# GpSimd copies of convolution weights, a last row point in written order, and another order of row points in a Winograd-style attention kernel

## The chip, the cores and the metric

The kernel runs on one core of a Trainium2 chip. The metric is the device time of one execution in microseconds (us), as the median of several runs. The core has engines with a queue each: TensorE (PE in the profile), VectorE (DVE), ScalarE (ACT), GpSimd (POOL), and SyncE (SP), which here issues most of the DMA transfers.

## The reference

The input x has 4 images of 256 channels and 64 x 64 pixels. A 7x7 convolution with dilation 2 (256 to 128 channels) and a 1x1 convolution (128 to 49) give 49 logits per pixel. A softmax over them weights the 49 shifted pixels of x. The sum is then whitened in groups of 64 channels over all images.

```python
k = lax.conv_general_dilated(x, w1, window_strides=(1, 1), padding=[(6, 6), (6, 6)], rhs_dilation=(2, 2), dimension_numbers=DN) + b1[None, :, None, None]
k = lax.conv_general_dilated(k, w2, window_strides=(1, 1), padding=[(0, 0), (0, 0)], dimension_numbers=DN) + b2[None, :, None, None]
attn = jax.nn.softmax(k, axis=1)
xp = jnp.pad(x, ((0, 0), (0, 0), (6, 6), (6, 6)))
shifts = jnp.stack([xp[:, :, 2 * u:2 * u + x.shape[2], 2 * v:2 * v + x.shape[3]] for u in range(7) for v in range(7)], axis=1)
return jnp.einsum('bkchw,bkhw->bchw', shifts, attn)
...
Sigma = EPS * I + jnp.einsum('gdm,gem->gde', xc, xc) / m
rTr = (1.0 / jnp.einsum('gii->g', Sigma))[:, None, None]
Sigma_N = Sigma * rTr
P = I
for _ in range(T_ITERS):
    P3 = jnp.einsum('gij,gjk,gkl->gil', P, P, P)
    P = 1.5 * P - 0.5 * jnp.einsum('gij,gjk->gik', P3, Sigma_N)
wm = P * jnp.sqrt(rTr)
xn = jnp.einsum('gde,gem->gdm', wm, xc)
```

## The kernel before

**The convolution.** The two convolutions are folded into one with 49 outputs, and that is computed in the manner of Winograd (Toom): in each direction the seven taps and the pixels are evaluated at seven points (0, 1, -1, 2, -2, one more, and infinity, which has the number 6 and the name `INF`), multiplied point by point, and interpolated. The outer loop runs over images and their *row points*, in the order of `ROWS` (L29). For one row point, the seven *column points* go in three groups, `BANKS` (L26): 1, 2, 0, then 3, 4, infinity, then 5. Each finite row point costs 96, 80 and 32 matmuls for the three banks; infinity has half the weights and so half the matmuls.

For one row point the steps are these. `row_eval` (L432) evaluates the pixels in the row direction on DVE (into one of three buffers `rb`), with some copies on ACT. `col_ops` (L466) evaluates that in the column direction into the tiles `xh`, one per column point, each of them single: the xh of the next row point can be written only when PE has read that of this one. `weights` (L361) makes the weights `wr0`, `wr1`, `wr2` of the banks: when a row point is used for the first time they are computed from the row-evaluated weights (DVE, with the points 0 and infinity as plain copies on ACT at L405, L406 and L415, and scalings on ACT at L428) and stored to `gd` in DRAM; after that they are loaded from `gd` by a DMA on SP's queue. The tiles wr0 to wr2 have one buffer each. The kept row-evaluated weights of row points 4, 5 and infinity come back by a DMA into `rb[0]`. `conv_bank` (L513) does the matmuls of one bank, and ACT copies their PSUM to `pv` (L541). `col_interp` (L602) interpolates `pv` in the column direction into `zz`, on DVE; `row_interp` (L633) interpolates the seven `zz` in the row direction into the logits `lgx`, in two parts: the first when all row points but the last are there, the second after the last.

`conv_step(k, i)` (L705) runs one bank: matmuls of row point k, then `prepare` (L697) for the same bank of row point k + 1, then the interpolation of k behind its last bank.

**Images.** Image 0 takes row points 1, 2, 3 and direct convolutions for the others; image 1 has infinity by a direct convolution and takes 0 to 5; images 2 and 3 take all seven. So the weights of rows 0, 4 and 5 are first made in image 1, and those of infinity in image 2.

**Softmax and attention.** While the convolution of image b runs, PE also does the softmax transposes of image b - 1 and the attention of an earlier image in *halves*: each has pixel transposes (L975, L1036), copies of them by ACT to `xb` (L983) and `yt` (L1044), and band matmuls (L1004). The softmax weights are exponentials on ACT (L860), maxima `mx`, reciprocals `s`, masks `rm` and products `d` on DVE (L852 to L873), copied to `zt` (L906), stored by SP to `sd` and loaded back as `band` (`load_band`, L937), which DVE transposes in place (L957). `plan` and `gap` (L1158 to L1210) place these between conv steps: a row of image b + 1 counts 6, 5 and 2 units for its banks (infinity half of that), and after each eighth of an image's units one gap's work is issued.

**What sets the order.** PE runs in the order in which the program is written (`pe` keeps it). The other engines' queues are ordered by a scheduler, with two means to fix it: `tc.high_priority()`, and `in_order()` (L293), under which the DVE instructions issued through `in_turn` (L280) form a strict chain and have high priority. The later part of a step can slip ahead of the earlier one where neither holds. Before, `in_order()` holds for the interpolation of row 4 (with the first part of `row_interp`) and of row 5, but not for `prepare`.

Of the kernel before, what the change touches and what calls it, by code (L numbers as in the profile page):

```python
# [23 lines left out]
INF = 6  # L24
# [1 line left out]
BANKS = ((1, 2, 0), (3, 4, 6), (5,))  # L26
ORDER = sum(BANKS, ())

ROWS = (INF, 0, 1, 2, 3, 4, 5)  # L29


@with_exitstack
def kernel(
# [29 lines left out]
    nc = tc.nc  # L63
    B, C, H, W = x.shape
# [24 lines left out]
    def taps(b):  # L89
        return (0,) if b == INF else (0, 1)  # L90
# [203 lines left out]
    @contextmanager  # L294
    def in_order():
        was = strict[0]
        strict[0] = True
        with tc.high_priority():
            yield
        strict[0] = was  # L300

    def add(o, a, b):
        return in_turn(TT(o, a, b, ALU.add))  # L303

    def sub(o, a, b):
        return in_turn(TT(o, a, b, ALU.subtract))  # L306

    def madd(o, a, f, b):

        return in_turn(STT(o, a, f, b, ALU.mult, ALU.add))  # L310
# [50 lines left out]
    def weights(b, br, i, mid=None):  # L361

        first = (br, i) not in made
        made.add((br, i))
        s0 = slot_of[BANKS[i][0]]
        ns = sum(len(taps(bc)) for bc in BANKS[i])  # L370
        nk = NSK * len(taps(br)) // 2
        wt = apool.tile([P, ns, NSK], F32, tag=f"wr{i}", name=f"wr_{b}_{br}_{i}")[:, :, :nk]
        w = {bc: wt[:, slot_of[bc] - s0 : slot_of[bc] - s0 + len(taps(bc))] for bc in BANKS[i]}
        if not first:
            nc.sync.dma_start(wt, gd[br][:, s0 : s0 + ns])
            return w

        if br == 0:
            g = [gr0[:, v] for v in range(KS)]
        elif br in kept:  # L380

            f = rb[0].rearrange("p q r c w -> p (q r c w)")[:, : KS * nk]
            if i == 0:
                nc.sync.dma_start(f, kept[br])
            f = f.rearrange("p (v a r k) -> p v a r k", v=KS, a=NCC, k=KT)
            g = [f[:, v] for v in range(KS)]
        else:
            g = [gbr[:, v] for v in range(KS)]
        g = [t.rearrange("p a r k -> p (a r k)") for t in g]

        e = ct.rearrange("p a b -> p (a b)") if b else store[4].rearrange("p c r w -> p (c r w)")
        e, o, e1 = (e[:, k * nk : (k + 1) * nk] for k in range(3))
        g0 = [g[KS - 1 - a] for a in range(4)]
        g1 = [g[KS - 5 - a] for a in range(3)]
        o0 = {bc: w[bc][:, 0] for bc in w}
        o1 = {bc: w[bc][:, 1] for bc in w if bc != INF}
        if i == 0:
            add(e, g0[0], g0[2])
            add(o, g0[1], g0[3])
            add(e1, g1[0], g1[2])  # L400
            add(o0[1], e, o)
            sub(o0[2], e, o)
            add(o1[1], e1, g1[1])
            sub(o1[2], e1, g1[1])
            nc.scalar.copy(o0[0], g0[0])  # L405
            nc.scalar.copy(o1[0], g1[0])  # L406
        elif i == 1:
            madd(e, g0[2], 4.0, g0[0])
            madd(o, g0[3], 4.0, g0[1])
            madd(e1, g1[2], 4.0, g1[0])  # L410
            madd(o0[3], o, 2.0, e)
            madd(o0[4], o, -2.0, e)
            madd(o1[3], g1[1], 2.0, e1)
            madd(o1[4], g1[1], -2.0, e1)
            nc.scalar.copy(o0[INF], g0[3])  # L415
        else:
            madd(o0[5], g0[0], 2.0, g0[1])
            madd(o1[5], g1[0], 4.0, g1[2])
            madd(o0[5], o0[5], 2.0, g0[2])
            if mid is not None:  # L420
                mid()
            madd(o1[5], g1[1], 2.0, o1[5])
            madd(o0[5], o0[5], 2.0, g0[3])
            add(o1[5], o1[5], o1[5])
        for bc in BANKS[i]:
            f = SCALE[bc] * (SCALE[br] if br not in kept else 1.0)
            if f != 1.0:
                nc.scalar.mul(w[bc], w[bc], f)  # L428
        nc.sync.dma_start(gd[br][:, s0 : s0 + ns], wt)
        return w  # L430

    def row_eval(b, br, rb=rb):  # L432

        for pr in range(2):
            xs = slots[2 * b + pr].rearrange("p c (q a) w -> p a q c w", a=4)
            r = [t[:, :, pr] for t in rb]
            if br == 1:
                add(r[0], xs[:, 0], xs[:, 2])
                add(r[1], xs[:, 1], xs[:, 3])
            elif br == 0:  # L440
                nc.scalar.copy(r[2], xs[:, 0])
            elif br == INF:
                nc.scalar.copy(r[1], xs[:, 3])
            X = [[xs[:, a, :, cc] for a in range(4)] for cc in range(NCC)]
            q = [[t[:, :, cc] for t in r] for cc in range(NCC)]
            for cc in range(NCC):
                if br == 3:
                    madd(q[cc][1], X[cc][2], 4.0, X[cc][0])
                    madd(q[cc][2], X[cc][3], 4.0, X[cc][1])
                elif br == 5:  # L450
                    madd(q[cc][2], X[cc][0], 2.0, X[cc][1])
            for a in (2, 3) if br == 5 else ():
                for cc in range(NCC):
                    madd(q[cc][2], q[cc][2], 2.0, X[cc][a])
        r = [t.rearrange("p q r c w -> p (q r c w)") for t in rb]
        if br == 1:
            add(r[2], r[0], r[1])
        elif br == 2:
            sub(r[0], r[0], r[1])
        elif br == 3:  # L460
            madd(r[0], r[2], 2.0, r[1])
        elif br == 4:
            madd(r[1], r[2], -2.0, r[1])
        return rb[{1: 2, 2: 0, 3: 0, 4: 1, 5: 2, 0: 2, INF: 1}[br]]
# [30 lines left out]
    def col_eval(src, i):  # L495
        for _ in col_ops(src, i):
            pass

    def both0(src, br, i):

        g = col_ops(src, i)
        next(g)
        nxt.update(weights(0, br, i, lambda: next(g)))
        for _ in g:
            pass
# [96 lines left out]
    def col_interp(b, br, part=None):  # L602
        at = slot[b, br]
        pt = {
            c: pv[:K2, at, i].rearrange("p q b -> p (q b)").rearrange(
                "p (q b two) -> p q b two", q=Q9, two=2
            )
            for i, c in enumerate(ORDER)
        }
        outs = phases(zz[:K2, br].rearrange("p q (w two) -> p q w two", two=2))  # L610
        cut = lambda t, k: t[:, :, k : k + Q8]
        if b > 0:

            t = pv[:K2, (at + 2) % NV, NP - 1].rearrange("p q b -> p (q b)")
        else:
            t = ct.rearrange("p a b -> p (a b)")[:K2, :PT]
        interpolate(
            pt, t.rearrange("p (q b two) -> p q b two", q=Q9, two=2), outs, cut, part
        )

        def end():
            ins = nc.scalar.copy(outs[3], cut(pt[5], 0))
            if br == INF:

                nc.gpsimd.memset(zz[:, INF, Q8], 0.0)
            return ins

        if part is None and b > 0 and br != ROWS[-2]:
            later.append(end)
        elif part != 0:  # L630
            end()
# [58 lines left out]
    nc.vector.memset(acc, 0.0)  # L690
    rows = [(0, br) for br in (1, 2, 3)]
    NR0 = len(rows)
    rows += [(b, br) for b in range(1, B) for br in ROWS[1 if b == 1 else 0 :]]
    cur, nxt = {}, {}

    def prepare(k, i):

        b, br = rows[k]
        w = weights(b, br, i)
        if i == 0:  # L700
            cur["x"] = row_eval(b, br)
        nxt.update(w)
        col_eval(cur["x"], i)

    def conv_step(k, i):  # L705
        w = {bc: nxt.pop(bc) for bc in BANKS[i]}
        b, br = rows[k]
        conv_bank(b, br, i, w)
        end = b > 0 and br == ROWS[-1]
        if end:  # L710

            with in_order():
                if i == len(BANKS) - 2:
                    col_interp(b, br, 0)
                elif i == len(BANKS) - 1:
                    col_interp(b, br, 1)
                    row_interp(b, 1)
        if k + 1 < len(rows):
            prepare(k + 1, i)
        if i == len(BANKS) - 1 and not end:  # L720
            last = br == ROWS[-2]
            with in_order() if last else nullcontext():
                col_interp(b, br)
                if last:
                    row_interp(b, 0)
# [24 lines left out]
    for i in three:  # L750
        nxt.update(weights(0, 1, i))
# [678 lines left out]
```

## Time and profile before

| | us |
|---|---|
| Median of 3 runs (lowest to highest) | 763.97 (761.77 to 764.57) |
| The profiled execution's own time | 761.8 |
| Its span, first to last instruction | 760.0 |
| PE busy | 698.6 (92%) |
| DVE busy | 643.0 (85%) |
| ACT busy | 342.8 (45%) |
| POOL busy | 33.7 (4%) |
| PE idle ahead of infinity bank 1 of image 2 (303.48) | 3.55 |
| PE idle ahead of infinity bank 2 of image 3 (460.68) | 7.34 |
| PE idle behind a late xb (277.62) | 4.32 |

The busy times and the span come from the profile of one execution, the idle times from its timeline. In a line of the timeline the first number is the start and the second the length, both in us, then come engine, line of the kernel, operation, output and inputs with their shapes, and in brackets the idle time of the engine before it with what ended that. A group of waits gives the same as a sum over the execution.

### The profile page before, as it was taken

The numbers are of one execution on the slowest core, as the hardware profiler recorded it, in microseconds if no ns is written. First come the engines' busy times: TensorE is split into PE (matmuls) and PEld (weight loads), VectorE is DVE, ScalarE is ACT, GpSimd is POOL, SyncE is SP. The second block draws the span as 40 slices with busy tenths as digits, with TensorE's granted clock in tenths as the row PEclk, the third lists the DMA queues.
The fourth block names the chain that finished last, engine by engine and source line by source line (L and its number), as shares of the span: only waits on it lengthen the run. The fifth ranks groups of instructions, "written<-read, shape, count | busy, mean of one in ns | idle before, by whom it ended". The sixth has DMA issues, their size and how long they took to land.

```text
span 760.0 us, 18845 instructions
## 1 busy us (share of the span) xinstructions
PE 698.6 (92%) x7608; PEld 539.3 (71%) x7608; DVE 643.0 (85%) x1394; ACT 342.8 (45%) x980; POOL 33.7 (4%) x45
## 2 busy tenths in 40 slices
PE   6999999996999877999999977999999889998996
PEld 1459643376998766888998967998898668885322
DVE  3799899999999989999994999999979675545665
ACT  1414240255355726366545442745435473322464
POOL 0410000020000010002000100000000000000000
PEclk9999999999899989999999998999999999999999
DMA  8981120227163563246745731342532134363488
GB/s 323 254 293 72 60 86 0 87 98 233 33 220 120 198 216 88 80 141 217 226 137 184 233 105 47 126 111 91 165 90 79 50 98 140 117 232 136 191 357 338
DMA packets 62911, 115.39 MB, mean 152 GB/s; under 512 B 26295, under 2 KB 45416, under 8 KB 62056
## 3 DMA queue, kind: packets, MB, share of 16 engines
q1 hardware_dynamic: 59128, 95.31, 38.4%
q0 software_dynamic: 3696, 18.88, 7.2%
q8 instruction: 60, 0.98, 0.6%
q14 instruction: 27, 0.22, 0.1%
HBM read 66.18 MB, written 47.98 MB: 150 GB/s over the span
## 4 chain that ended last, share of the span: by engine, by line
DVE 44%; PE 41%; ACT 5%; DMA 4%; issue 4%; SPq 1%; DVEq 0%; ACTq 0%
PE cv L531 9%; PE y L1004 8%; PE acc L668 6%; DVE xh L310 6%; DVE pv L310 5%; DVE rb L310 4%; PE tp L1370 4%; DVE ct L310 3%; DVE band L957 3%; DVE ct L303 3%; DVE zz L310 3%; DVE pv L306 2%; PE tp L1036 2%; PE tp L975 2%; PE sig L1057 2%
## 5 line engine op out<-in xcount | busy, mean ns | idle before, releaser
L531 PE MATMUL cv<-xh,wr 128*49 128x128 f32 (+1 forms) x4576 | 268.8, 279 | 19.5 <-issue 7.3
L531 PEld LDWEIGHTS cv<-xh,wr 128*49 128x49 f32 x4576 | 260.6, 126 | 25.5 <-issue 18.0
L1004 PE MATMUL y<-band,xb 128*128 128x224 f32 (+2 forms) x640 | 151.2, 374 | 15.0 <-ACT xb L983 12.9
L1004 PEld LDWEIGHTS y<-band,xb 128*128 128x128 f32 x640 | 109.6, 193 | 36.4 <-ACT xb L983 16.0
L541 ACT COPY pv<-cv 113x486 f32<-113x486 f32 (+1 forms) x69 | 33.2, 483 | 101.8 <-PE cv L531 101.5
L1023 ACT ACTIVATE slot<-y,pivot 128x512 f32<-128x512 f32 x53 | 36.8, 741 | 62.1 <-PE y L1004 62.1
L310 DVE SCALAR_TENSOR_TENSOR pv<-pv 113x162 f32<-113x162 f32 x215 | 63.8, 318 | 0.5
L1044 ACT COPY yt<-tp 128x256 f32<-128x256 f32 x128 | 45.9, 379 | 36.3 <-PE tp L1036 35.2
L957 DVE STREAM_TRANSPOSE band<-band 128x960 f32<-128x960 f32 (+1 forms) x48 | 50.9, 1060 | 9.9 <-DMA band<-sd 9.9
L1036 PE MATMUL tp<-ident,slot 128*128 128x128 f32 x256 | 52.0, 299 | 4.4 <-ACT yt L1044 2.3
L975 PE MATMUL tp<-ident,slot 128*128 128x128 f32 x256 | 50.5, 300 | 4.6 <-ACT yt L1044 4.5
L1036 PEld LDWEIGHTS tp<-ident,slot 128*128 128x128 f32 x256 | 41.3, 205 | 13.3 <-issue 3.2
L975 PEld LDWEIGHTS tp<-ident,slot 128*128 128x128 f32 x256 | 40.4, 206 | 11.0 <-ACT yt L1044 6.0
L906 ACT COPY zt<-d 32x112 f32<-32x112 f32 (+2 forms) x156 | 45.0, 289 | 1.8
L860 ACT ACTIVATE d<-tp,mx 128x49 f32<-128x49 f32 x128 | 37.5, 335 | 14.0 <-DVE mx L855 10.7
L310 DVE SCALAR_TENSOR_TENSOR xh<-ct 128x512 f32<-128x512 f32 x46 | 30.3, 683 | 10.2 <-PE cv L531 10.2
L1057 PE MATMUL sig<-yt 128*64 128x65 f32 x1024 | 36.9, 225 | 0.0
L1057 PEld LDWEIGHTS sig<-yt 128*64 128x64 f32 x1024 | 32.5, 137 | 6.0 <-issue 4.5
L983 DVE COPY xb<-tp 128x256 f32<-128x256 f32 x41 | 16.4, 421 | 23.7 <-PE tp L975 23.7
L983 ACT COPY xb<-tp 128x256 f32<-128x256 f32 x87 | 30.4, 376 | 12.7 <-PE tp L975 12.0
L306 DVE TENSOR_TENSOR pv<-pv 113x162 f32<-113x162 f32 x112 | 34.6, 319 | 0.4
L668 PE MATMUL acc<-slot,tap 128*49 128x496 f32 (+3 forms) x168 | 34.6, 569 | 0.0
(221 smaller groups left out, 947.2 us busy)
## 6 DMA issues: line engine op xcount, KB each, us to landing
out_dram<-out SPq DMA_DIRECT2D x32, 512.0 KB, 3.4
sd<-zt SPq DMA_DIRECT2D x16, 896.0 KB, 4.2
slot<-in_x_dram POOLq DMA_DIRECT2D x12, 1024.0 KB, 9.2
band<-sd SPq DMA_DIRECT2D x128, 84.0 KB, 2.2
wr<-gd SPq DMA_DIRECT2D x15, 588.0 KB, 3.8
wr<-gd SPq DMA_DIRECT2D x15, 490.0 KB, 3.5
spill<-slot POOLq DMA_DIRECT2D x3, 2048.0 KB, 8.4
back<-spill SPq DMA_DIRECT2D x3, 2048.0 KB, 12.8
```

What stands on the lines that cost most here:

```text
L306: return in_turn(TT(o, a, b, ALU.subtract))
L310: return in_turn(STT(o, a, f, b, ALU.mult, ALU.add))
L531: nc.tensor.matmul(cv[h * HB : h * HB + KT, k, sr : sr + n, sc : sc + n], wv[:, sc, sr, cc], xh[bc][:, :n, h * NCC + cc, :n], start=(j == ...
L668: nc.tensor.matmul(ps[h * HB : h * HB + KT, :, w0:w1_], w[v][:, cc], xs[:, :, cc, w0 + d : w1_ + d], start=(j == 0), stop=(j == len(order) ...
L906: ins = nc.scalar.copy(o, i)
L957: nc.vector.transpose(f, f)
L975: nc.tensor.transpose(t[:, cc * P : (cc + 1) * P], xt[:, cc, CR * m : CR * (m + 1), bass.ds(pc, SW, 2)], ident,)
L983: (nc.vector.tensor_copy if tail else nc.scalar.copy)(xb, t[:, :C])
L1004: nc.tensor.matmul(ps[:, cc, q0 - half * HALF : q1 - half * HALF, :], xb[:, cc * P : (cc + 1) * P], rhs, start=(k == 0), stop=(k == len(PI ...
L1036: nc.tensor.transpose(t[:, cc * P : (cc + 1) * P], yt[:, cc, CR * i : CR * (i + 1), bass.ds(pc, SW, 2)], ident,)
L1044: nc.scalar.copy(yb.rearrange("p a g c -> p (a g) c")[:, :, :GW], t[:, :C].rearrange("p (e c) -> p e c", c=GW),)
L1057: nc.tensor.matmul(sig[g * GW : (g + 1) * GW, cc], yb[:, cc, g, :GW], yb[:, cc, g], start=(count[0] == 0 and cc == 0), stop=(count[0] == 4 ...
```

## The change

The change has three parts. `ROWS` begins with row point 0 and has infinity second; image 1 still leaves infinity out, so its own order (0, 1, 2, 3, 4, 5) stays, and images 2 and 3 take 0, infinity, 1, 2, 3, 4, 5 where they took infinity, 0, 1, 2, 3, 4, 5. The plain copies of weights are issued on GpSimd in images 1 and later, and stay on ScalarE in image 0. And `prepare` for row point 5, banks 1 and 2, is put under `in_order()` in images 1 to 3: these instructions join the strict chain, so that they stand ahead of the interpolation of row 4, which is issued after them.

```diff
-ROWS = (INF, 0, 1, 2, 3, 4, 5)
+ROWS = (0, INF, 1, 2, 3, 4, 5)
...
+
+        same = nc.scalar.copy if b == 0 else nc.gpsimd.tensor_copy
         if i == 0:
...
-            nc.scalar.copy(o0[0], g0[0])
-            nc.scalar.copy(o1[0], g1[0])
+            same(o0[0], g0[0])
+            same(o1[0], g1[0])
         elif i == 1:
...
-            nc.scalar.copy(o0[INF], g0[3])
+            same(o0[INF], g0[3])
...
-    rows += [(b, br) for b in range(1, B) for br in ROWS[1 if b == 1 else 0 :]]
+    rows += [(b, br) for b in range(1, B) for br in ROWS if (b, br) != (1, INF)]
...
         if k + 1 < len(rows):
-            prepare(k + 1, i)
+
+            with in_order() if b > 0 and br == ROWS[-2] and i > 0 else nullcontext():
+                prepare(k + 1, i)
```

## The prediction

> **What bounds the kernel now.** I read the page first, for the engines' shares and the chain that ended last.
>
> ```profile
> PE 698.6 (92%) x7608; PEld 539.3 (71%) x7608; DVE 643.0 (85%) x1394; ACT 342.8 (45%) x980; POOL 33.7 (4%) x45
> ...
> DVE 44%; PE 41%; ACT 5%; DMA 4%; issue 4%; SPq 1%; DVEq 0%; ACTq 0%
> ```
>
> PE is busy 92% of the span, yet the chain lies on DVE as often as on PE: the limit changes from stage to stage. ACT has room. So I asked next for busy time in stretches around the places that the change touches.
>
> ```profile
> 280.00:300.00 20.00, 18.42 (x226) 16.41 (x222) 16.87 (x48) 11.61 (x27) 0.00 (x0) 0.92 0.22 49
> 300.00:340.00 40.00, 35.45 (x462) 33.00 (x463) 40.00 (x82) 21.36 (x76) 0.15 (x1) 0.96 0.38 115
> ...
> 400.00:420.00 20.00, 19.47 (x282) 17.79 (x280) 9.37 (x16) 10.68 (x29) 0.57 (x1) 1.00 0.59 210
> 420.00:460.00 40.00, 31.72 (x410) 28.08 (x406) 39.00 (x84) 17.97 (x37) 3.38 (x2) 0.97 0.51 145
> 460.00:480.00 20.00, 19.32 (x238) 18.22 (x240) 19.97 (x40) 6.18 (x17) 0.00 (x0) 0.90 0.15 42
> ```
>
> The columns are length, then busy time of PE, weight loads, DVE, ACT and POOL, clock, DMA share and GB/s. Around the change of image (image 2 begins at about 297 us, image 3 at about 447) DVE is full and PE has holes. From 400 to 420 it is the reverse. The timeline of PE shows the holes.
>
> ```profile
> 277.62 1.17 PE L1004 MATMUL y<-band,xb 128*128 128x96 f32 x4 [4.32 <-ACT xb L983]
> ...
> 303.48 4.12 PE L531 MATMUL cv<-xh,wr 128*49 128x128 f32 x40 [3.55 <-DVE xh L310]
> ...
> 323.38 12.11 PE L531 MATMUL cv<-xh,wr 128*49 128x128 f32 x208
> ```
>
> The last line is rows 0 (banks 1 and 2) and 1 (bank 0) of image 2 in one go: 80 + 32 + 96 matmuls. The first 112 take 12.11 x 112/208 = 6.5 us, so row 1 of image 2 starts at about 330.0. Image 3 has the like hole (7.34 us, before 460.68), and its row 1 starts at 477.33 + 11.80 x 112/208 = 483.7. The timelines of ACT and DVE show who holds whom:
>
> ```profile
> 276.85 0.27 ACT L405 COPY wr<-rb 128x98 f32<-128x98 f32 x1 [5.10 <-DMA rb<-gi]
> ...
> 277.20 0.36 ACT L983 COPY xb<-tp 128x256 f32<-128x256 f32 x1
> ```
> ```profile
> 282.94 1.18 DVE L957 STREAM_TRANSPOSE band<-band 128x960 f32<-128x960 f32 x1 [3.52 <-DMA band<-sd]
> ...
> 329.22 0.63 DVE L303 TENSOR_TENSOR xh<-ct 128x512 f32<-128x512 f32 x1
> ...
> 416.54 0.69 DVE L310 SCALAR_TENSOR_TENSOR xh<-ct 128x512 f32<-128x512 f32 x1 [6.30 <-PE cv L531]
> ...
> 481.64 0.68 DVE L303 TENSOR_TENSOR xh<-ct 128x512 f32<-128x512 f32 x1
> ```
>
> ACT's weight copy for infinity waits 5.10 us for the kept weights; the copy of xb behind it comes late, PE idles 4.32 us, and the band that follows is late for DVE (3.52 us). After that DVE runs without a hole, and the first xh of row 1 is ready at 329.8 (image 2) and 482.2 (image 3), just when PE needs it. What the change is worth is therefore how far it moves these two starts; from each of them on the PE order of both kernels is the same and DVE is some 6 to 11 us ahead.
>
> [...]No run here shows a 128x196 copy on POOL; the nearest row is the swap copy 128x64, two in 0.41 us.[...]
>
> **Part 1, copies to POOL.** Twelve copies leave ACT: rows 0, 4 and 5 of image 1 (nine of 128x196, .36 to .38 us each) and infinity of image 2 (three of 128x98, .27): 9 x .37 + 3 x .27 = 4.1 us of ACT. ACT is 45% busy, so that itself is worth nothing, except where a copy holds the queue: the 5.10 us wait now stands on POOL, where only a spill and slot loads stand near it (issued at 258.96 and 268.07, ahead of infinity's copies). It gives back up to 3.5 us on DVE plus a .19 us band wait at 299.76: 3.7. On POOL I estimate .27 us for a copy 128x196 and .18 for 98 wide. Row 0's three fall near 100 us, where PE is full (39.08 of 40 from 60 to 100) and covers them. The other nine (6 x .27 + 3 x .18 = 2.2) fall where DVE is the limit[...]. I take .4, as the copies wait for the same DMA as DVE's first weight instruction and mostly overlap waits.
>
> **Part 2, row 0 first.** No instruction is added or removed in images 2 and 3. PE now runs row 0 (banks 0, 1), the attention half and softmax transposes, row 0 bank 2, infinity (48 + 40 + 16 matmuls), then row 1. Row 1's evaluation (four of 1.13 us and one of 2.2), and the softmax pieces mx, s, rm and d of the image before, now come on DVE between infinity's and row 1's xh. Adding up every DVE instruction from row 5 of image 1 to row 1 of image 2 by its duration from the timeline gives 72.0 us before and 72.3 after: +.3. So the hole of PE ahead of infinity bank 2 isn't filled: it moves ahead of row 1, and is about 10 us there, since PE then has less conv work (infinity, half as wide) ahead of it. Row 1's start is still DVE's queue.
>
> New waits stand in that queue, all bounded by zero below: mx waits for the softmax transposes, which PE reaches later than DVE does (0 to .9 us, from PE's transposes ending near 309.8 in my schedule); the second reciprocal waits for exponentials that stand on ACT behind eleven zt copies (3.40 us in one group) and an eviction (0 to 1.1); bands of the next half wait for a transfer (0 to 1.9 for two). One more band transpose (1.09) now stands between row 1's first and second xh; PE needs the second 1.8 us (32 matmuls at 12.11/208 = .058) after the first, so it is just covered (.6 + 1.1 = 1.7); if its load is late, every us of it shows.
>
> **Part 3, row 5 in strict order.** The evaluation for row 5, banks 1 and 2, is put on the written order in images 1 to 3, ahead of the interpolation of row 4. It adds waits: xh is single, so its bank 2 must wait for PE to have read that of row 4, and the interpolation, bands and row_interp queue behind it. Before, those pieces slipped in between. Image 1: 0 to 1.0 us (bank 2 of row 4 ends near 262.7). Image 2: it falls in the stretch where DVE is idle half the time (9.37 of 20) and PE full; nothing, and without that cover some .5. Image 3 has no row after row 5, so its own end isn't touched.
>
> **Sum.** Image 2's row 1: -3.7 (wait gone) + .3 (order) + .4 (POOL) + half to all of the new waits, of 4.9 in all (.9 + 1.1 + 1.9 + 1.0); I take 3.4: +.4. Image 3: the strict wait .4, mx and reciprocal .4 to .9 each at half: from 0 to +1.0; +.5. Total about +.9: the profiled execution, 761.8 (span 760.0 and 1.8 around it), would become 762.7. The median of the runs shown is 2.2 above that execution, so 764.9 in its terms, no change that can be told: 0.5%, 3.8 us, is about what a measurement can tell.
>
> **Rivals.** *Faster, the holes are reclaimed.* If none of the new waits appears and PE's earlier start on image 2 lets the bands arrive early, image 2 gains the full 3.7 and about 1 us of strict order (row 5's conv starting earlier in image 1, where PE idles 2.22 us at 254); image 3, whose 1.0 us of DVE idling from 420 to 460 goes, .8 more: -5.5, 758.5. For it: the waits of before are measured, the new ones estimated. Against it: DVE is full from 300 to 400 and 420 to 540, and a full queue can't be shortened by order. *Much faster*: DVE's queue isn't what sets row 1, and the 4.3 and 7.3 us of PE become conv work: -11.6, 752.4. Against: xh at 329.22 and 481.64 ends where PE starts.
>
> *Slower, a band takes the place of the wait.* SP issues the bands in order behind weight loads and stores that wait for PE; wr tiles are single, so row 1's weight load waits for infinity's conv. The band transpose between row 1's two xh then waits on SP's queue, in one of the two images. The point: my schedule has DVE there at 331.0 and the load landing at 328.3; from 2.7 us later on each us shows. At the 3.5 us of the present band wait, on top of the sum: +.9 + 3.5 + 2.2[...] = +6.6, 770.6. *The change doesn't do what it says*: POOL copies issued late (strict order behind the spill, which waited 85.7 us) would stall the weights; the order on POOL has row 5's ahead of that spill, so I give it little.
>
> **How the numbers follow.** Forecast 764.9: chance .50 (761 to 768). Reclaimed: .22; much faster: .05; band: .18; late POOL copies or others: .05. Range: leaving out the much faster and half of the late cases, 757.5 to 770.6. Faster by over 0.5%: .22 + .05 = .27 (758.5 is 5.5 below the median). Slower: .18 + .05 = .23. Same: .50.
>
> **What would show it.** Right: ACT's line with the 5.10 us wait for gi is gone, with PE's 4.32 and DVE's 3.52; the 3.55 and 7.34 us holes of PE are gone and one of some 10 us stands ahead of row 1 in images 2 and 3; DVE stays full there. POOL copies near .27 us; DVE instructions beside them lengthened by under .3. Wrong: row 1 of image 2 or 3 starts over 3 us from 330.0 and 483.7 (less image 1's shift); a new wait of DVE on a band after 320; or DVE under 38 us busy of 40 in these stretches.

## The result and the profile after

The changed kernel takes 773.25 us (773.12 to 774.04), the kernel before 763.50 in the same session: 1.0131 times as long, 95% interval 1.0113 to 1.0149, some 10 us. The profiled execution has a span of 771.5 us where that of before had 760.0. The first part of the page, and the chain that ended last, of the changed kernel:

```profile
PE 699.7 (91%) x7608; PEld 539.6 (70%) x7608; DVE 646.9 (84%) x1394; ACT 340.3 (44%) x968; POOL 55.3 (7%) x57
...
PE 47%; DVE 36%; DMA 6%; ACT 5%; issue 4%; SPq 1%; DVEq 0%; ACTq 0%
```

The work is nearly the same: PE is busy 1.1 us longer than before and DVE 3.9, and ACT loses 2.5 us. Most of the 11.5 us is idle time. Busy times by stretch (length, then PE, weight loads, DVE, ACT, POOL, clock, DMA share, GB/s), four of the changed kernel and then the first and the last of them before, show where:

```profile
260.00:280.00 20.00, 18.58 (x259) 16.98 (x260) 15.18 (x39) 9.91 (x28) 3.91 (x3) 1.00 0.98 343
280.00:300.00 20.00, 16.47 (x201) 14.85 (x198) 18.09 (x38) 8.43 (x18) 0.00 (x0) 0.91 0.29 79
300.00:320.00 20.00, 18.70 (x252) 17.14 (x250) 19.79 (x51) 11.38 (x38) 1.32 (x3) 1.00 0.12 30
320.00:340.00 20.00, 6.60 (x90) 5.87 (x88) 18.82 (x40) 8.83 (x36) 0.00 (x0) 0.70 0.42 133
...
260.00:280.00 20.00, 15.68 (x199) 14.06 (x199) 19.35 (x39) 8.82 (x26) 3.38 (x2) 0.91 0.92 325
...
320.00:340.00 20.00, 19.64 (x282) 18.31 (x281) 20.00 (x40) 14.54 (x59) 0.15 (x1) 1.00 0.35 116
```

From 260 to 280 DVE now idles for 4.8 us, and from 320 to 340 PE works 6.6 us of 20. Before, the same stretches had DVE at 19.35 and PE at 19.64. The timeline of PE after has the holes where row 1 begins; its first line is row 4's bank 2, followed by other matmuls, in image 1:

```profile
261.97 7.27 PE L533 MATMUL cv<-xh,wr 128*49 128x128 f32 x128
...
327.19 1.36 PE L533 MATMUL cv<-xh,wr 128*49 128x128 f32 x16 [4.41 <-ACT wr L430]
337.55 7.42 PE L533 MATMUL cv<-xh,wr 128*49 128x128 f32 x96 [8.99 <-DVE xh L303]
...
493.52 7.92 PE L533 MATMUL cv<-xh,wr 128*49 128x128 f32 x96 [9.66 <-DVE xh L303]
```

Row 1 of image 2 starts at 337.55 (330.0 before), that of image 3 at 493.52 (483.7 before). The old holes of 4.32, 3.55 and 7.34 us are gone or smaller, and holes of 9 and 10 us stand ahead of row 1. Ahead of the first of them PE also waits 4.41 us for infinity's bank 2, whose weights ACT scales late. The timeline of DVE, after, says what made xh late:

```profile
264.02 0.63 DVE L310 SCALAR_TENSOR_TENSOR wr<-rb 128x196 f32<-128x196 f32 x2 [3.01 <-issue]
...
267.68 1.18 DVE L961 STREAM_TRANSPOSE band<-band 128x960 f32<-128x960 f32 x1 [1.33 <-DMA band<-sd]
...
270.43 0.33 DVE L306 TENSOR_TENSOR pv<-pv 113x162 f32<-113x162 f32 x1
270.80 0.33 DVE L303 TENSOR_TENSOR pv<-pv 113x162 f32<-113x162 f32 x1
...
283.15 1.18 DVE L961 STREAM_TRANSPOSE band<-band 128x960 f32<-128x960 f32 x1 [1.71 <-PE cv L533]
...
326.92 0.20 DVE L868 RECIPROCAL s<-s 128x8 f32<-128x8 f32 x1 [1.18 <-ACT d L864]
...
336.81 0.69 DVE L303 TENSOR_TENSOR xh<-ct 128x512 f32<-128x512 f32 x1
...
492.73 0.68 DVE L303 TENSOR_TENSOR xh<-ct 128x512 f32<-128x512 f32 x1
```

The first line is the first instruction of row 5's bank 2 (its weights are in `wr2`). It waits 3.01 us, and the profile names nothing that ended the wait ("issue"). The time points to the weight tile that PE frees when it ends row 4's bank 2: that group of PE starts at 261.97 and takes 7.27 us for 128 matmuls, 32 of them bank 2, so these end at about 263.8, and DVE goes on .23 us later. The store of the old weights to `gd`, which reads the same tile, had landed at 248.2. The same place before, where nothing waits and the interpolation of row 4 (`pv`) is mixed in:

```profile
265.83 0.32 DVE L306 TENSOR_TENSOR pv<-pv 113x162 f32<-113x162 f32 x1
266.07 0.35 DVE L310 SCALAR_TENSOR_TENSOR wr<-rb 128x196 f32<-128x196 f32 x1
266.35 0.32 DVE L310 SCALAR_TENSOR_TENSOR pv<-pv 113x162 f32<-113x162 f32 x1
```

After, two bands come late, 1.33 and 1.71 us. (The line at 283.15 names PE, whose group ends at 283.06; the last of that band's transfers landed at 283.03, so either may have held it.) In between, the interpolation of row 4 stands bare (113x162, from 270.07 to 275.89): where an instruction overwrites an input of the one just before it, or needs its result, the two started .35 to .37 us apart there, and .22 to .25 where neither is so. Before, from 255.32 to 258.31, with other work in between, each instruction started .23 to .27 us after the one ahead.

To compare runs, I cut the execution at five points of DVE's timeline: A from row 5's first weight instruction in image 1 (247.54 before) to the last instruction of the first part of image 1's row_interp (285.21); B to row 1's first xh of image 2 (329.22); C to the same point of image 2 (440.30); D to row 1's first xh of image 3 (481.64); E to the end. What comes ahead of A is left out: in some profiled executions the first image's pixels arrive late, and those of e6, e8 and e15 reach A 4.4, 9.9 and 5.3 us later than that of before. Differences to before, in us, worked out from the timelines (good to about .1):

| kernel | A | B | C | D | E | sum |
|---|---|---|---|---|---|---|
| changed | +5.0 | +2.5 | +1.9 | +1.6 | +0.4 | +11.4 |
| changed, once more (e5) | +4.8 | +2.4 | +2.2 | +1.8 | +0.4 | +11.6 |
| strict order only (e1) | +4.4 | -0.3 | +1.9 | +0.6 | -1.9 | +4.6 |
| row order only (e2) | +0.9 | +2.3 | +0.7 | -1.3 | +1.2 | +3.8 |
| copies only (e3) | -1.0 | +1.3 | 0.0 | 0.0 | +0.1 | +0.4 |
| rows, copies (e4) | +2.7 | +2.7 | +0.9 | +0.3 | -0.1 | +6.4 |
| all, strict for bank 1 (e6) | +2.3 | +2.1 | +0.9 | +1.4 | +1.3 | +8.0 |
| rows, strict (e7) | +5.8 | +3.8 | +1.8 | +1.0 | +0.4 | +12.8 |
| copies, strict (e8) | +5.2 | -0.3 | +1.5 | +0.7 | -1.8 | +5.3 |
| copies, half load (e9) | -3.2 | -0.3 | 0.0 | +0.1 | +2.0 | -1.4 |
| rows, copies, late gap (e10) | +0.7 | -0.6 | +0.8 | -0.8 | +0.4 | +0.6 |
| the same (e16) | +2.1 | -0.6 | +2.3 | -1.5 | +2.8 | +5.1 |
| all, strict for bank 2 (e13) | +4.5 | +2.4 | +2.1 | +1.8 | +0.4 | +11.3 |
| all, late gap (e14) | +4.7 | -0.2 | +5.0 | -0.7 | +1.1 | +10.0 |
| rows, infinity's copies, late gap (e15) | +0.7 | -0.2 | +0.9 | -0.6 | +1.5 | +2.3 |
| late gap only (e11) | +0.7 | -1.6 | +7.7 | -2.4 | +6.0 | +10.4 |
| infinity's copies, late gap (e12) | +0.5 | -2.7 | +9.3 | -2.4 | +6.0 | +10.6 |

Profiles of one kernel differ by up to 2.4 us in a stage (e10 and e16), so only larger differences, or such as come back in several kernels, carry weight.

Stage A holds the same 83 DVE instructions in both kernels. Of its 5.0 us, 3.1 are idle time (6.7 against 3.7): the new wait of 3.0 and some .6 in very short gaps of the bare chain, while the waits for bands are 3.0 in place of 3.5. The other 1.9 is the instructions' own time: about 1.5 for the bare chain (e1, with the strict order alone, has it) and .4 beside the GpSimd copies (e3 has it). Stage B has 108 instructions where it had 101, which take 1.1 us longer, and 1.3 us more of idle time.

### The profile page after: what moved, and what is told of

It reads as the page before. It is cut to its first block, busy times and chain, and to the rows that moved or that the text cites. A ratio compares the mean times of both kernels' runs of the same rounds, so it can differ in the third digit from the quotient of the medians.

```text
span 771.5 us, 18859 instructions
## 1 busy us (share of the span) xinstructions
PE 699.7 (91%) x7608; PEld 539.6 (70%) x7608; DVE 646.9 (84%) x1394; ACT 340.3 (44%) x968; POOL 55.3 (7%) x57
## 4 chain that ended last, share of the span: by engine, by line
PE 47%; DVE 36%; DMA 6%; ACT 5%; issue 4%; SPq 1%; DVEq 0%; ACTq 0%
PE cv L533 13%; PE y L1008 10%; PE acc L670 6%; DVE xh L310 4%; DVE rb L310 4%; PE tp L1374 4%; DMA band<-sd 4%; DVE pv L310 3%; DVE ct L310 3%; DVE zz L310 3%; DVE band L961 3%; PE tp L1040 3%; PE tp L979 3%; PE sig L1061 3%; DVE ct L303 2%
## 5 line engine op out<-in xcount | busy, mean ns | idle before, releaser
L1008 PE MATMUL y<-band,xb 128*128 128x224 f32 (+2 forms) x640 | 151.2, 375 | 12.8 <-ACT xb L987 10.1
L1008 PEld LDWEIGHTS y<-band,xb 128*128 128x128 f32 x640 | 109.3, 193 | 34.3 <-ACT xb L987 12.9
L1027 ACT ACTIVATE slot<-y,pivot 128x512 f32<-128x512 f32 x53 | 36.7, 739 | 56.4 <-PE y L1008 56.4
L864 ACT ACTIVATE d<-tp,mx 128x49 f32<-128x49 f32 x128 | 37.3, 330 | 11.5 <-DVE mx L859 8.1
```

Source lines behind the costliest of these rows:

```text
L864: nc.scalar.activation(d[:, h, i], lt[i // NI][:, i % NI, h, :KT], AF.Exp, bias=mx[:, i, h : h + 1], accum_out=s[:, h, i : i + 1],)
L1008: nc.tensor.matmul(ps[:, cc, q0 - half * HALF : q1 - half * HALF, :], xb[:, cc * P : (cc + 1) * P], rhs, start=(k == 0), stop=(k == len(PI ...
```

## The experiments

**The parts alone.** e1 has the strict order only, e2 the row order only, e3 the copies only, e4 rows and copies.

```diff
 e1: -ROWS = (0, INF, 1, 2, 3, 4, 5)
     +ROWS = (INF, 0, 1, 2, 3, 4, 5)
     -        same = nc.scalar.copy if b == 0 else nc.gpsimd.tensor_copy
     +        same = nc.scalar.copy
 e4: -            with in_order() if b > 0 and br == ROWS[-2] and i > 0 else nullcontext():
     +            with nullcontext():
```

Against the changed kernel, e1 so undoes the row order and the copies, and e4 undoes the strict order. In the same way e2 undoes the copies and the strict order, and e3 the row order and the strict order.

> Only row point 5 in written order; row points and copies as before. Theory A (the strict order is the main cost: DVE stops where it used to slip interpolation in, at the single wr2 and xh tiles, about 5 us in image 2 and 1 in image 3): 764 + 6 = 770 us, with idle DVE near 261 us of 3 us ahead of the bank 2 weights of row 5. Theory B (the order of row points is the main cost): 764, within 1.5.

Measured 766.82 us, ratio 1.0030 (1.0012 to 1.0048). Dearer than theory B, cheaper than A's 770; the place is A's, in the timeline of DVE of e1:

```profile
264.48 0.64 DVE L310 SCALAR_TENSOR_TENSOR wr<-rb 128x196 f32<-128x196 f32 x2 [3.63 <-issue]
...
267.96 1.18 DVE L961 STREAM_TRANSPOSE band<-band 128x960 f32<-128x960 f32 x1 [1.76 <-DMA band<-sd]
```

> Only row 0 ahead of infinity in images 2 and 3. Theory A: new waits of the second reciprocal and mx and 0.3 us more work ahead of row 1, 2.5 us in image 2 and 1.6 in image 3: 768 us. Theory B: 773 us, row 1 of images 2 and 3 late by 7 and 10 us.

767.34 us, 1.0022 (1.0006 to 1.0039). Stage B is +2.3 as A had it, but image 3 gains in D. Theory B's 773 is out.

> Only the weight copies on GpSimd. Theory A: the 5.1 us wait of ACT for infinity's weights goes, PE's 4.3 us hole behind it and DVE's 3.5 us band wait with it; a few tenths of contention: 760.5 us. Rival C ([...]DVE loses what GpSimd takes, some 2 us, and a copy that comes late holds up weights): 764 to 767.

764.39 us, 0.9994 (0.9978 to 1.0010): no gain. ACT's 5.1 us wait and PE's hole of 4.3 us were gone, and yet DVE's wait for bands stayed, in two pieces (timeline of DVE, e3):

```profile
282.87 1.18 DVE L961 STREAM_TRANSPOSE band<-band 128x960 f32<-128x960 f32 x1 [2.08 <-DMA band<-sd]
...
295.02 0.85 DVE L961 STREAM_TRANSPOSE band<-band 128x640 f32<-128x640 f32 x1 [1.46 <-DMA band<-sd]
```

2.08 + 1.46 = 3.54 us, against 3.52 + .19 before. What PE had lost at 273 it now lost at 285 (5.06 us, for xh). The rival's contention is there too, and small: the group of four rb instructions beside a POOL copy took 2.93 instead of 2.48 us (2.78 in the changed kernel), one of four pv instructions 1.33 instead of 1.03, .75 together.

> The changed kernel without the strict order. Theory A: 773 less 5 to 6 us: 767.5 us. Theory B: 773, no different from the changed kernel.

768.15 us, 1.0046 (1.0029 to 1.0062), near theory A. So the strict order costs the changed kernel most, some 6 us on top of these two, and more than the 2.3 us that it costs alone.

**Which part of the strict order, and with what.** e5 is the changed kernel again, e7 has the copies back on ACT, e8 the old row order; e6 and e13 restrict the strict order to one bank.

```diff
 e6:  -            with in_order() if b > 0 and br == ROWS[-2] and i > 0 else nullcontext():
      +            with in_order() if b > 0 and br == ROWS[-2] and i == 1 else nullcontext():
 e13: -            with in_order() if b > 0 and br == ROWS[-2] and i > 0 else nullcontext():
      +            with in_order() if b > 0 and br == ROWS[-2] and i == 2 else nullcontext():
```

> The changed kernel once more, as the measure for the others of this group. 1.0113 to 1.0149 times the kernel before, some 773 us.

773.98 us, 1.0123 (1.0098 to 1.0149).

> The changed kernel with the strict order for bank 1 of row 5 only; bank 2 is free as before. Theory A' (bank 2 in strict order is what costs: DVE arrives at 260.9 us, PE has read bank 2 of row 4 only at 263.8, and the interpolation queues behind; the idle 3.0 us and the bare interpolation chain go): 4 us below the changed kernel, 769, with no idle DVE ahead of the bank 2 weights. Rival (any strict order costs, since the scheduler can't mix the interpolation with it): within 1 us of the changed kernel.

772.84 us, 1.0101 (1.0073 to 1.0130) with six executions from 769 to 775: the 769 of theory A' wasn't met, and by the median the rival stands as well. The fastest of the six took 769.27 us, that of nine of the changed kernel 773.12. The stages tell the two apart: A is 40.0 us and not 42.5, C as without strict order, and DVE doesn't stop ahead of bank 2's weights. The profiled execution had 4.4 us of late pixels ahead of A. The timeline of DVE of e6 has only bands late there:

```profile
271.38 1.18 DVE L961 STREAM_TRANSPOSE band<-band 128x960 f32<-128x960 f32 x1 [1.03 <-DMA band<-sd]
...
289.08 1.18 DVE L961 STREAM_TRANSPOSE band<-band 128x960 f32<-128x960 f32 x1 [3.65 <-DMA band<-sd]
```

> The changed kernel with the weight copies back on ACT. If the copies on GpSimd matter little here, 772 to 774 us. If the two parts by themselves (1.003 and 1.002) only add up, 768 us, and the copies are what makes the rest.

775.36 us, 1.0142 (1.0111 to 1.0174): the loss doesn't need the copies, and row order and strict order together cost far more than the sum of the two alone.

> The changed kernel with the old order of row points. If the parts add up (strict order 2 to 5 us, copies 0 to 1.3): 766 to 770 us. If the strict order costs more where the copies are on GpSimd: 771 us or more.

768.26 us, 1.0066 (1.0035 to 1.0098): within the range for parts that add up. By stages it is their sum (5.3 against 4.6 and 0.4); by the medians it is some 5 us against 2.

> The changed kernel with the strict order for bank 2 of row 5 only. Stages from the first weight of row 5: theory A' (bank 2 waits for PE's conv of row 4's bank 2, and the interpolation behind it): the stage to the end of row_interp of image 1 is 42.5 us as in the changed kernel, against 40.0 with bank 1 alone and 40.4 with neither; idle DVE of about 1 to 3 us ahead of bank 2's weights. Rival (the two banks together cost): about 41.

776.08 us, 1.0143 (1.0117 to 1.0169). All stages are those of the changed kernel within .5 us, and the wait is back (timeline of DVE, e13):

```profile
264.44 0.64 DVE L310 SCALAR_TENSOR_TENSOR wr<-rb 128x196 f32<-128x196 f32 x2 [3.12 <-issue]
```

Bank 2 in strict order carries the cost in stage A. The seven profiles that have it show A at 42.0 to 43.5 us, the others, e9 apart, at 36.7 to 40.4. In all seven this instruction waits, for 3.01 to 3.89 us, and starts .23 or .24 us after 32/128 of PE's group; in none of the others does it wait.

**What makes the band late.** The DMA view of before for 255 to 300 us, in 40 equal slices (busy tenths of the DMA engines), with two of the issues of that stretch (KB each, us from issue to landing):

```profile
DMA  9217999979992569999999410000000340091770
...
spill<-slot POOLq DMA_DIRECT2D x1, 2048.0 KB, 8.4
slot<-in_x_dram POOLq DMA_DIRECT2D x2, 1024.0 KB, 10.5
```

From 259 to 280 us the DMA engines are mostly full with a spill and a slot load of 2 MB each. The second half of that load lands at 282.27; transfers of the late band, issued from 272.7 to 274.0, land from 282.46 to 282.82, and DVE goes on at 282.94. e9 is e3 with half of that load left out (its later results are then of wrong pixels, so it is no version to keep):

```diff
         for cc in range(NCC):
             ...
+            if k == 5 and cc:
+                continue
             queue.dma_start(store[s][:, cc], src[:, :, pr, :])
```

> The kernel with only the copies on GpSimd, and the load of image 2's second half of rows into its slot (2 MB, issued about 270 us) left out for channels 128 to 255, so that the logits of image 2 and all after are of wrong pixels; 1 MB less moves just then. Theory F (the band that DVE waits for is late because the DMA engines are full from 260 to 280 us, not because ACT waited): the band wait of 2.1 us near 283 falls under 0.5 us and the stage from the first weight of row 5 to the end of row_interp of image 1, 36.7 us, to about 34.5; 761 us. Rival (the band is late for its place on SP's queue or for PE's last read of the old band): unchanged, 764.

762.09 us, 0.9953 (0.9932 to 0.9974) of before, by the ratios 3 us under e3. Stage A is 34.5 us as theory F had it, and no band wait is left in A or B. The band in the timeline of DVE of e9:

```profile
280.46 1.17 DVE L963 STREAM_TRANSPOSE band<-band 128x960 f32<-128x960 f32 x1
```

The same band's transfers land at 278.30 to 278.73 where in e3 they land at 282.40 to 282.75. So the late band hangs on the load beside it; whether it shares the engines with the load or queues behind it these runs don't tell apart. Taking ACT's copy away could not bring it.

**The order of row points.** In e10, e11, e12, e14, e15 and e16 the first gap of images 2 and 3 comes later:

```diff
-            if at * NPC >= (j + 1) * whole:
+            if at * NPC >= (j + 1) * whole and not (b > 1 and j == 0 and at < 19.5):
```

> No strict order; rows and copies as changed; the first gap of images 2 and 3 (attention half and softmax of the image before) comes after 19.5 units of conv work, behind infinity, instead of 11. Theory G (row order costs because the softmax pieces stand in DVE's queue ahead of row 1): row 1 of images 2 and 3 starts 1 to 2.5 us earlier each than with the first gap at 11, stage from row_interp to row 1's xh 44.5 instead of 46.7 us; 765.5 us against 768. Rival (it costs for the waits of xh and weights only): no gain, 768.

768.07 us with four executions from 763.0 to 770.5, 1.0072 (1.0043 to 1.0100), by time the rival's number; once more with 22:

> Rows and copies as changed, no strict order, late gap, once more for a better interval: 0.998 to 1.003 times the kernel before by the stages of its profile, 763 to 766 us; if the 1.007 of its four runs is right, 769.

767.07 us, 1.0019 (1.0002 to 1.0036), some 2 us below e4's 1.0046, though the two intervals still overlap. The stages say it more clearly: B is 43.4 us in both, against 46.7 with the gap at 11 units, and D 40.6 and 39.9 against 41.7. The timeline of DVE of e10 has row 1's first xh of image 2 5.5 us earlier than e4, of which 2.2 come from stage A, ahead of the gap that was moved, and are scatter:

```profile
286.48 0.75 DVE L303 TENSOR_TENSOR zz<-ct,zz 113x576 f32<-113x576 f32 x1
...
329.92 0.68 DVE L303 TENSOR_TENSOR xh<-ct 128x512 f32<-128x512 f32 x1
```

> The changed kernel, its strict order too, with the first gap of images 2 and 3 at 19.5 units. If gap and strict order are independent: stage from row_interp to row 1's xh of image 2 falls from 46.5 to about 43.5 and the like in image 3 by 1 to 2.5 us, 768 us, while the 42.5 us stage of the strict order stays.

770.03 us, 1.0059 (1.0032 to 1.0087): about half of the loss comes back. A stays at 42.4, B falls by 2.7 and D by 2.3 against the changed kernel, as expected; C, in its one profile, grows by 3.2: eight more DVE instructions stand there (1.6 us), and DVE waits 10.7 us for xh of row 5 where it waited 6.3, less the 2.4 us by which bands are earlier.

> The kernel before, with the first gap of images 2 and 3 after 19.5 units (behind row 0) instead of 12.5. Theory G: mx, s and rm (1.2 us) no longer stand ahead of row 1's xh: 1 us less in each of two images, 762 us. Rival (the attention half fills a hole ahead of infinity's bank 2 only): 764 to 766.

772.33 us, 1.0120 (1.0094 to 1.0146), a clear miss of both theories. B and D fall, by 1.6 and 2.4: DVE has row 1's xh earlier. But PE now has the attention half directly ahead of row 1, and reaches it at 333.45 where the xh was ready at 329.6; and the hole of 7.35 us ahead of infinity's bank 2 in image 3 is as long as before. C grows by 7.7 and E by 6.0, in e12 by 9.3 and 6.0; what of that comes from these two stays open. The late gap pays only with row 0 first.

> As the one before it, with infinity's three weight copies on GpSimd (rows 0, 4 and 5 on ACT). If the 1.0 us that the copies gave in the stage around 280 us is had without the 0.75 us that the others took from DVE: 761 us. If not: as the one before it.

770.69 us, 1.0101 (1.0071 to 1.0131): as e11.

> Rows as changed, no strict order, late gap, and only infinity's three copies on GpSimd. 0.75 us less contention than with all twelve: 762 us; if it beats both kernels, by 1 to 2 us under the kernel before. If the copies of rows 4 and 5 on GpSimd also relieved ACT: as the next one, 764.

765.41 us, 1.0008 (0.9992 to 1.0024): no different from the kernel before. No version that computes the same was clearly faster than it.

## Why the prediction was wrong

The forecast of 764.9 and its range up to 770.6 were too low; the direction "slower" had .23. Point by point:

**Part 3 is where the sum failed.** The step was "Image 1: 0 to 1.0 us (bank 2 of row 4 ends near 262.7)" and, for image 2, "nothing". Stage A costs 5.0, and e6, e13 and e1 put it on bank 2. I had the right wait and missized it twice. PE ended that bank at 263.8 (263.3 in the trace of before, where I had read 262.7), and DVE stood there already at 261.0: the interpolation of row 4, which used to fill this time, is what the strict order put behind the wait, so the arrival has to be counted without it. That makes the wait 3.0 us. And I priced the wait alone, not the bare chain that follows where everything that could be mixed in had been done: about 2 us, 1.5 in instructions that start further apart and some .6 in short gaps. In image 2 the cover that I named, a DVE idle half of the time, lies ahead of the point. C is 1.0 to 1.9 us longer with the strict order than without it, in each of the four pairs (changed and e4, e7 and e2, e8 and e3, e1 and before). In the changed kernel 1.6 of its 1.9 us are idle time, most of it at bands, which cost DVE 6.2 us there in place of 4.9.

**Part 1 failed in its gain.** The step "It gives back up to 3.5 us on DVE" took the band's lateness for a result of ACT's wait. The two stood one behind the other in the chain, but e3 and e9 show the band's transfer held by the load beside it: in the changed kernel the bands of stage A still cost 3.0 us where they cost 3.5. What PE gained at 273 was lost again within 20 us. The contention taken at .4 was .75 for two groups in e3; in the changed kernel the copies 128x196 took .35 to .82 us, two long ones apart, and not .27 (98 wide: .27 to .75, not .18). The .4, .27 and .18 were my estimates: the only POOL copies of before are two of 128x64, .41 us together, at 596.76.

**Part 2 held in kind.** The hole was to move ahead of row 1 and be "about 10 us": 8.99 and 9.66. DVE's queue sets row 1. The second reciprocal's wait was bounded at 1.1 and measured 1.18 and 1.16; mx in image 3 at .48, within .9; the band between row 1's two xh was covered. B came out at +2.5 where order, mx and reciprocal taken at half gave 1.3: the order, put at .3, is 1.1 for seven instructions more ahead of row 1, and the reciprocal reached its bound. e10 and e16 take 3.3 of B away, from e4's 46.7, by moving the softmax pieces, with the attention half, behind infinity.

**The rivals.** "Much faster" fell as argued, and "reclaimed" with the gain of part 1. The slower one named a late band, behind weight loads on SP's queue that wait for PE (134.5 us in all before, 12.9 at most), but between row 1's xh; there it wasn't late. The bands that were late are 60 us earlier.

**What stays open.** Row order and strict order together cost 10 to 11 us by the medians (e7), alone 1.7 and 2.3; so the larger part of the loss, some 7 us, comes only when both are there. By the stages it is less, 12.8 against 3.8 and 4.6, some 4 us, most of it in B, D and E. No run isolates this interplay, and why medians and profiles disagree about the parts isn't shown. Fastest execution against fastest of the same session, e1 stands 3.8 us above the kernel before, e2 3.6 and e7 12.4, which is near the profiles; with 4 to 75 executions on a side that is a rough measure.

## What to carry to other kernels

Before putting instructions in a strict order, ask what waited behind them and what filled the time until their tile came free: the work pushed behind a waiting instruction is lost as filler and then runs bare (here 3.0 us of wait and about 2 of bare chain). A wait that stands next to another in the chain need not be its effect; look at what else is being transferred just then. And where a queue is full, moving work on another engine can just move the hole (here PE's 4.32 us ahead of 277.62; in the changed kernel 1.11, 1.04 and 2.50 us up to 294.10), unless something leaves the stretch ahead of the instruction that is awaited.

## What the runs showed of the hardware

Two POOL copies 128x196 of the changed kernel took 13.82 and 3.03 us, where the other seven took .35 to .82. The first one (timeline of POOL):

```profile
97.19 13.82 POOL L407 COPY wr<-lgx 128x196 f32<-128x196 f32 x1 [52.85 <-ACT lgx L788]
110.95 0.45 POOL L408 COPY wr<-lgx 128x196 f32<-128x196 f32 x1
```

and DVE of the same kernel when it ended:

```profile
108.08 2.48 DVE L310 SCALAR_TENSOR_TENSOR slot<-slot,slot 128x512 f32<-128x512 f32 x4
110.49 0.31 DVE L303 TENSOR_TENSOR ct<-pv 113x162 f32<-113x162 f32 x1
110.83 0.35 DVE L306 TENSOR_TENSOR pv<-pv 113x162 f32<-113x162 f32 x1
```

From 96.36 on DVE ran one instruction behind the other, each starting some .08 us before the one ahead ended. The copy, .45 us for its twin, ended only at 111.01, after some 20 of them: the instruction at 110.83, which overwrites an input of the one before it, is the first with a gap ahead of it (.03 us), and that gap begins .21 us before the copy's end. DVE lost nothing in this: the same four instructions took 2.49 us before.

The coincidence comes back. In e3 the same copy takes 13.82 us as well. Row 5's third copy, at another place, takes 3.03 us in the changed kernel and 3.30 in e3, and ends .22 and .21 us after a gap of .03 us in DVE's work begins. In e3 the first copy of infinity's weights, 2.73 us where the next two take .27, ends .13 us after DVE's wait of 2.08 us for a band begins. But the copy at 229.71 of the changed kernel took .81 us while DVE had no gap. No run moved a gap alone, so what held the long copies isn't shown. Nothing needed the first copy so early: after the copies, the next instruction on its tile is one of DVE at 142.62.
